# A graph network in three gather passes: blocks of many and of few columns set alternately

## Chip, cores and metric

The kernel runs on one core of a Trainium2 chip. The metric is the device time of one launch in microseconds (us); smaller is better. The core has five engines that run side by side: TensorE (PE in the profile, its weight loads PEld), VectorE (DVE), ScalarE (ACT), GpSimd (POOL) and SyncE (SP). GpSimd issues the gathers, SyncE most plain transfers.

## What is computed

A directed graph has 6250 nodes with 256 features each and 100000 edges sorted by target `dst`. Two GATv2 layers (4 heads of 64) with self loops, a residual and layer norm, then one GAT layer (8 heads of 32), again with residual and layer norm. Cut to what matters:

```python
def _gatv2_layer(x, src, dst, n, Wl, Wr, att, b):
    xl = (x @ Wl).reshape(n, H, C)
    xr = (x @ Wr).reshape(n, H, C)
    e = leaky_relu(xl[src] + xr[dst], 0.2)
    logits = einsum('ehc,hc->eh', e, att)
    alpha = softmax of logits over the edges of each dst
    return segment_sum(xl[src] * alpha[:, :, None], dst) + b
h = elu(gatv2(x, ...)); h = gatv2(h, ...); x = layernorm(x + h)
# GAT: Wh = x @ W, e = leaky_relu(s1[src] + s2[dst]), softmax over dst, weighted sum
x = layernorm(x + gat(x))
```

The costly part is `xl[src]` three times: a row of about 1 KB for each of 100000 edges in each layer.

## The kernel before

`make_plan` counts the edges of each node and sorts the nodes by falling degree. The place of a node in that order (`place`) is split into a partition (`place & 127`, `piece[:, 0]`) and a block (`place >> 7`, `piece[:, 1]`): 49 blocks of 128 nodes, one node to a partition. Since the nodes of a block have about the same degree, a block needs only as many *columns* (edges of a node, gathered side by side) as its largest node has. The function `columns` fixes these numbers from the expected distribution of degrees. They are, by block: 38, 25, 24, 23, 22, 21, 21, 20, 20, 20, 19 x4, 18 x4, 17 x4, 16 x5, 15 x5, 14 x5, 13 x4, 12 x3, 11, 11, 10, 10, 9. Block 0 is gathered with 27 columns, its few longer nodes in an extra gather (`few_row`). The sum over the blocks is 803 columns in each layer.

`tile_by_degree` then makes three passes over the 49 blocks. Passes 1 and 2 are `layer2(0, ...)` and `layer2(1, ...)`, pass 3 is the code behind them. For each block b a pass does, in the order of the program:

- `gather(b + 1)`: one indirect DMA on GpSimd for each column of the next block (line 1235). It fetches 128 rows of 1040 to 1056 bytes, one to a partition, from a table in HBM (`xl1_d`, `xl2_d` or `wh_d`; in the profile `xl_d` and `whs_d`). Their targets are tiles `g` of up to T = 9 rows, from a pool of nine buffers (`rowp`). A GATv2 block takes its columns and one own row, cut by `chunks` in equal parts of at most nine: 18 columns or more make three tiles (four for block 0), 17 or fewer make two. GpSimd works through this list in order. It stops where a tile's buffer is still in use by the block that held it nine tiles earlier. In pass 1 it also fetches node features for block b + 3 (line 1595).
- `ready(b + 1)`: the products of the block's own rows (pass 1) or a copy of rows loaded before (pass 2).
- `attend(b)`: VectorE makes the logits, three instructions for each tile (lines 1504 to 1506: max, product, sum), and the top (line 1374). ScalarE exponentiates (line 1381).
- `end(b - 1)`: VectorE takes the finished sum `acc` of the block before, from PSUM (line 1537), and normalizes it.
- reciprocal of the new denominators (line 1571; it comes once per block and is used below as the block's mark).
- `weighted_sum`: VectorE multiplies the tiles by the weights (line 1411). ScalarE does so for the last third of the columns, with one instruction for each column and head (line 1410). TensorE adds all columns up in PSUM by products with an identity (line 1418). Only then are the tiles free again.
- the rest of `finish` for block b - 1: transposes, products, and a write of the table rows for the next layer by SyncE.

In pass 3 the logits are short, and VectorE does the weighted sum too (lines 1433 and 1442); GpSimd writes the output rows with one indirect DMA for each block (line 1733).

At the end of a pass, `begin` gathers the first 14, 12 and 11 columns of blocks 0 to 2 of the next pass. It reads only rows of the first 45 blocks (`AHEAD`), so that it need not wait for the last four (`LATE = 4`). For this `sort_sources` sorts the sources of blocks 0 to 2 by place. Everything in `tile_by_degree` takes its number of columns from the list `cols` by block number and the nodes from the places.

Of the kernel before, what the change touches and what calls it, by code (L numbers as in the profile page):

```python
# [28 lines left out]
I32 = mybir.dt.int32  # L29
AF = mybir.ActivationFunctionType  # L30
OP = mybir.AluOpType
# [4 lines left out]
P = 128  # L36
# [4 lines left out]
RUNS = 64  # L41
EARLY = (14, 12, 11)
LATE = 4


def columns(E, N, NB):

    mean = E / N
    pmf = [math.exp(-mean)]
    for k in range(1, 200):
        pmf.append(pmf[-1] * mean / k)
    over, sd = [], []
    for c in range(199):
        p = sum(pmf[c + 1 :])
        g = sum((k - mean) * pmf[k] for k in range(c + 1, 200))
        over.append(N * p)  # L60
        sd.append(math.sqrt(max(N * (p * (1.0 - p) - g * g / mean), 0.0)))
    cols = []
    for b in range(NB):
        most = P * b
        cols.append(next(
            c for c in range(199) if (over[c] + 3.5 * sd[c] <= most if b else over[c] < 0.01)
        ))
    low = max((c for c in range(199) if N - over[c] <= P // 4), default=0)
    high = next(c for c in range(199) if over[c] <= P // 4)
    pmf += [0.0] * 200  # L70
    held = next(
        c for c in range(199)
        if N * sum((k - c) * pmf[k] for k in range(c, 200))
        + 3.5 * math.sqrt(N * sum((k - c) ** 2 * pmf[k] for k in range(c, 200))) <= P
    )
    assert cols[1] <= held < cols[0]
    return cols, low, high, held


@with_exitstack  # L80
# [566 lines left out]
def kernel(  # L647
# [20 lines left out]
    NB = -(-N // P)  # L668
    NP = NB * P
    cols, low, high, held = columns(E, N, NB)  # L670
    CM = max(cols)
    H2, D2 = att1.shape
# [18 lines left out]
    with tc.manual_schedule():  # L691
        make_plan(
            tc, x, src, dst, ((wl1, wr1, att1), (wl2, wr2, att2)), (b1, b2), w3, a3,
            cols, low, high, held, node_i, fits, ident, eps, nobody, att, wc, wh, fixed, xl1_d, near_d,
        )
        nc.vector.memset(done, 0)
# [18 lines left out]
def make_plan(  # L715
# [6 lines left out]
    nc = tc.nc  # L722
    N, F = x.shape
    E = src.shape[0]
    NB = node_i.shape[1]
# [12 lines left out]
    one = ctx.enter_context(tc.tile_pool(name="plan_one", bufs=1))  # L738
# [306 lines left out]
    place_f = one.tile([P, NB], F32, name="place_f")  # L1045
# [3 lines left out]
    piece = one.tile([P, 2, NB], I32, name="piece")  # L1049
    nc.vector.tensor_single_scalar(piece[:, 0, :], place, P - 1, op=OP.bitwise_and)  # L1050
    nc.vector.tensor_single_scalar(piece[:, 1, :], place, 7, op=OP.logical_shift_right)
    nc.vector.tensor_scalar(vals[:, 2, :], count, 255.0, None, op0=OP.min)
    to = one.tile([P, 2, NB], BF16, name="to")
    nc.vector.tensor_copy(to, piece)
# [88 lines left out]
def tile_by_degree(  # L1143
# [32 lines left out]

    AHEAD = (NB - LATE) * P
    KEY = max(cols).bit_length()
# [614 lines left out]
```

## Time and profile before

| what | value |
|---|---|
| time, median of 3 runs | 3889.89 us (3889.52 to 3891.73) |
| profiled execution | 3880.55 us |
| its span, first to last instruction | 3878.7 us |
| VectorE busy | 2836.2 us (73%) |
| GpSimd busy | 2530.5 us (65%) |
| TensorE busy, weight loads | 1481.8 us (38%), 1113.8 us (29%) |
| ScalarE busy | 1091.1 us (28%) |
| gathers of layers 1 and 2 | 1569 of 948 ns, 766 of 1036 ns in layer 3, and 2 x 37 early ones |
| data moved | 395.60 MB, 102 GB/s |
| mean granted TensorE clock | 0.665 |

The span has four parts. The plan and the first table last until 150 us. Pass 1 then runs until about 1500 us, pass 2 until about 2710 us, and pass 3 to the end. In lines of the profile, idle time of an engine stands behind the bar or in brackets, with what ended it. "issue" means that the profile shows nothing that it waited for; "remote" means that the releaser is not known. The times of TensorE's ends are modelled. The rows here come from one execution, whose own time is 3880.55 us.

### The profile page before, as it was taken

The page shows a single profiled execution, that of the slowest core. Times are in us where ns is not written, and L with a number is a line of the kernel's source. Part 1 is how long each engine was busy: PE and PEld are TensorE (multiplying, and loading weights), DVE is VectorE, ACT ScalarE, POOL GpSimd, SP SyncE. Part 2 cuts the span into 40 slices and gives each one's busy share as a digit, 9 for nine tenths or more (in the row PEclk, how much of TensorE's full clock was granted, in tenths as well). Part 3 has the DMA queues.
Part 4 walks back from the last instruction along what each step waited for, and adds up shares of the span by engine and source line. Part 5 has one row for each costly group of instructions (what it writes and reads, how often), then busy time and mean ns, then how long its engine had stood idle before and what let it go on. Part 6 is the DMA issues. An engine that isn't in the chain of part 4 may idle for free.

```text
span 3878.7 us, 23608 instructions
## 1 busy us (share of the span) xinstructions
PE 1481.8 (38%) x5130; PEld 1113.8 (29%) x5130; DVE 2836.2 (73%) x2648; ACT 1091.1 (28%) x4176; POOL 2530.5 (65%) x2613
## 2 busy tenths in 40 slices
PE   6324665556667763355544545554000000000000
PEld 5213444434555542343433433443000000000000
DVE  6228988668888876899876988896676565666665
ACT  3113444334445442243433434443000000000000
POOL 6464666666666645666666666664777777777774
PEclk8656877778788886676666677776555555555555
DMA  8532333333434334333433434442343333333332
GB/s 188 109 92 78 98 104 104 100 99 103 105 102 108 104 79 109 100 106 104 112 107 105 111 107 110 109 111 74 101 108 101 96 97 96 97 97 96 97 97 57
DMA packets 196123, 395.60 MB, mean 102 GB/s; under 512 B 63036, under 2 KB 115514, under 8 KB 195956
## 3 DMA queue, kind: packets, MB, share of 16 engines
q0 software_dynamic: 122048, 338.04, 33.2%
q1 hardware_dynamic: 66226, 54.22, 5.1%
q10 hardware_dynamic: 7698, 1.74, 0.4%
q8 instruction: 45, 0.74, 0.1%
q14 instruction: 106, 0.87, 0.1%
HBM read 353.82 MB, written 40.42 MB: 102 GB/s over the span
## 4 chain that ended last, share of the span: by engine, by line
issue 20%; POOL 20%; DVE 13%; PE 10%; another core or an unknown queue 6%; ACT 5%; DMA 1%; DVEq 0%; POOLq 0%; ACTq 0%
POOL g L1235 18%; PE acc L1418 6%; DVE z L1505 4%; DVE z L1504 4%; DVE lg L1506 3%; PE pm L1362 3%; ACT g L1410 2%; ACT wt L1381 2%; DVE g L1411 1%; POOL out L1733 1%; DMA g<-xl_d,near_r 1%; DVE weighted L1433 1%; ACT xT L1357 0%; PE pt L1355 0%
## 5 line engine op out<-in xcount | busy, mean ns | idle before, releaser
L1235 POOL DMA_INDIRECT g<-xl_d,near_r x1569 | 1487.4, 948 | 858.7 <-issue 454.3
L1418 PE MATMUL acc<-g,ident 128*128 128x256 f32 x3408 | 1015.9, 461 | 765.3 <-issue 282.7
L1418 PEld LDWEIGHTS acc<-g,ident 128*128 128x128 f32 x3408 | 774.4, 234 | 1004.2 <-issue 522.3
L1235 POOL DMA_INDIRECT g<-whs_d,near_r x766 | 793.2, 1036 | 284.2 <-issue 250.0
L1410 ACT ACTIVATE g<-g,by 128x64 f32<-128x64 f32 x2056 | 545.1, 337 | 316.1 <-issue 310.8
L1504 DVE TENSOR_TENSOR z<-g,pr 128x1820 f32<-128x1820 f32 (+4 forms) x234 | 497.1, 2125 | 19.1 <-DMA g<-xl_d,near_r 10.0
L1505 DVE TENSOR_TENSOR z<-z,at 128x1820 f32<-128x1820 f32 (+4 forms) x234 | 497.4, 2126 | 8.0
L1506 DVE TENSOR_REDUCE lg<-z 128x28 f32<-128x1820 f32 (+4 forms) x234 | 497.3, 2125 | 8.1
L1442 DVE TENSOR_REDUCE acc_v<-weighted 128x256 f32<-128x4096 f32 (+15 forms) x49 | 343.7, 7014 | 16.5 <-remote 8.3
L1411 DVE TENSOR_TENSOR g<-g,wt 128x1792 f32<-128x1792 f32 (+8 forms) x234 | 348.4, 1505 | 2.9
L1391 ACT ACTIVATE wt<-lg 128x128 f32<-128x128 f32 (+17 forms) x49 | 14.0, 285 | 851.0 <-DVE top L1374 391.5
L1703 DVE TENSOR_TENSOR lg<-g,s_r 128x56 f32<-128x56 f32 (+4 forms) x111 | 22.1, 213 | 315.1 <-DMA g<-whs_d,near_r 272.5
L1357 ACT COPY xT<-pt 128x256 f32<-128x256 f32 x147 | 54.9, 374 | 688.5 <-remote 342.2
L1433 DVE TENSOR_TENSOR weighted<-g,wt 128x1792 f32<-128x1792 f32 (+4 forms) x111 | 226.6, 2056 | 0.1
L1571 DVE RECIPROCAL den<-den 128x4 f32<-128x4 f32 x98 | 17.4, 177 | 212.9 <-ACT wt L1381 165.2
L1381 ACT ACTIVATE wt<-lg,top 128x19 f32<-128x19 f32 (+14 forms) x392 | 116.0, 296 | 190.8 <-DVE lg L1506 74.3
L1362 PE MATMUL pm<-wcat,xT 128*128 128x260 f32 x392 | 136.0, 505 | 56.3 <-ACT xT L1357 49.8
L1362 PE MATMUL pm<-wh_cat,xT 128*128 128x272 f32 x196 | 77.5, 531 | 183.8 <-ACT xT L1357 95.5
L1537 DVE TENSOR_TENSOR h<-acc,den 128x256 f32<-128x256 f32 x98 | 40.7, 416 | 126.2 <-remote 112.8
L1362 PEld LDWEIGHTS pm<-wcat,xT 128*128 128x128 f32 x392 | 94.8, 255 | 90.5 <-ACT xT L1357 64.6
L1362 PEld LDWEIGHTS pm<-wh_cat,xT 128*128 128x128 f32 x196 | 42.8, 242 | 203.0 <-ACT xT L1357 104.7
L1362 PE MATMUL pl<-wcat,xT 128*128 128x260 f32 x196 | 64.0, 455 | 55.5 <-issue 40.4
(232 smaller groups left out, 1548.4 us busy)
## 6 DMA issues: line engine op xcount, KB each, us to landing
g<-xl_d,near_r POOLq DMA_INDIRECT x1569
g<-whs_d,near_r POOLq DMA_INDIRECT x766
whs_d<-row SPq DMA_DIRECT2D x49, 132.0 KB
xl_d<-xl SPq DMA_DIRECT2D x49, 130.0 KB
xl_d<-row SPq DMA_DIRECT2D x49, 130.0 KB
xr_d<-row SPq DMA_DIRECT2D x49, 130.0 KB
two<-xl_d SPq DMA_DIRECT2D x49, 130.0 KB
two<-xr_d SPq DMA_DIRECT2D x49, 130.0 KB
```

What stands on the lines that cost most here:

```text
L1235: nc.gpsimd.indirect_dma_start(out=g[:, j + own - s0, :width], out_offset=None, in_=table, in_offset=source(of, b, j),)
L1357: nc.scalar.copy(xT, pt)
L1362: nc.tensor.matmul(pm, xT[:, c, :], w[:, c, :], start=c == 0, stop=c == 1)
L1381: nc.scalar.activation(wt[:, :, h], lg[:, :S, h], AF.Exp, bias=top[:, h : h + 1], accum_out=den[:, h : h + 1],)
L1410: nc.scalar.mul(g4[:, t, h, :], g4[:, t, h, :], by[:, t - m, h : h + 1])
L1411: nc.vector.tensor_mul(g4[:, :m], g4[:, :m], wt[:, s0 : s0 + m, :].unsqueeze(3).to_broadcast([P, m, H, F // H]),)
L1418: nc.tensor.matmul(acc, ident, g4[:, t], start=s0 + t == 0, stop=s0 + t == S - 1 and not more)
L1433: nc.vector.tensor_mul(prod[:, s0 - base : s1 - base, :].rearrange("p t (h d) -> p t h d", h=H), g[:, :n, :F].rearrange("p t (h d) -> p t ...
L1442: nc.vector.reduce_sum(part, prod[:, : s1 - base, :].rearrange("p s f -> p f s"), axis=AX.X)
L1504: nc.vector.tensor_max(z, g[:, :n, :W2], xr[:, None, :].to_broadcast([P, n, W2]))
L1505: nc.vector.tensor_mul(z, z, at[:, None, :].to_broadcast([P, n, W2]))
L1506: nc.vector.reduce_sum(lg[:, s0:s1, :], z.rearrange("p t (h d) -> p t h d", h=H2), axis=AX.X)
```

## The change

After the columns are worked out, the list is permuted: blocks 0 to 2 and the last four stay where they are. The 42 blocks between are laid out with a large and a small one by turns. By number of columns the order becomes 38, 25, 24, 23, 11, 22, 12, 21, 12, 21, 12, 20, 13, 20, 13, 20, 13, 19, 13, 19, 14, 19, 14, 19, 14, 18, 14, 18, 14, 18, 15, 18, 15, 17, 15, 17, 15, 17, 15, 17, 16, 16, 16, 16, 16, then 11, 10, 10, 9 as before. `make_plan` applies the same permutation to the block number of each node with ten small VectorE instructions, so that the places, and all tables written by place, follow. The blocks themselves (which nodes, how many columns, how many tiles) are the same, and nothing else is edited.

```diff
+FIRST = len(EARLY)
...
-    return cols, low, high, held
+    turns = cols[:]
+    for r in range(FIRST, NB - LATE):
+        turns[min(2 * r - FIRST, 2 * (NB - LATE) - 1 + FIRST - 2 * r)] = cols[r]
+    return turns, low, high, held
...
     nc.vector.tensor_single_scalar(piece[:, 1, :], place, 7, op=OP.logical_shift_right)
+    turn_a = one.tile([P, NB], I32, name="turn_a")
+    turn_b = one.tile([P, NB], I32, name="turn_b")
+    nc.vector.tensor_scalar(
+        turn_a, piece[:, 1, :], 2.0, float(-FIRST), op0=OP.mult, op1=OP.add
+    )
+    nc.vector.tensor_scalar(
+        turn_b, piece[:, 1, :], -2.0, float(2 * (NB - LATE) - 1 + FIRST), op0=OP.mult, op1=OP.add
+    )
+    nc.vector.tensor_tensor(turn_a, turn_a, turn_b, op=OP.min)
+    nc.vector.tensor_tensor(turn_a, turn_a, piece[:, 1, :], op=OP.subtract)
+    nc.vector.tensor_single_scalar(turn_b, piece[:, 1, :], float(FIRST), op=OP.is_ge)
+    nc.vector.tensor_tensor(turn_a, turn_a, turn_b, op=OP.mult)
+    nc.vector.tensor_single_scalar(turn_b, piece[:, 1, :], float(NB - LATE), op=OP.is_lt)
+    nc.vector.tensor_tensor(turn_a, turn_a, turn_b, op=OP.mult)
+    nc.vector.tensor_tensor(piece[:, 1, :], piece[:, 1, :], turn_a, op=OP.add)
+    nc.vector.scalar_tensor_tensor(
+        place_f, piece[:, 1, :], float(P), piece[:, 0, :], op0=OP.mult, op1=OP.add
+    )
```

## The prediction

> **What bounds the kernel now.** I read the page first, then the waits of GpSimd and VectorE pass by pass, then the timeline of a few blocks. The page:
>
> ```profile
> PE 1481.8 (38%) x5130; PEld 1113.8 (29%) x5130; DVE 2836.2 (73%) x2648; ACT 1091.1 (28%) x4176; POOL 2530.5 (65%) x2613
> L1235 POOL DMA_INDIRECT g<-xl_d,near_r x1569 | 1487.4, 948 | 858.7 <-issue 454.3
> L1235 POOL DMA_INDIRECT g<-whs_d,near_r x766 | 793.2, 1036 | 284.2 <-issue 250.0
> ```
>
> A gather costs GpSimd 0.95 us and 0.30 us until the next, so 1.25 us. VectorE is the busiest and GpSimd next; neither fills the span. The waits of GpSimd between 1567 and 2617 us (pass 2, the gathers of blocks 3 to 47) and of VectorE between 2773 and 3720 us (pass 3):
>
> ```profile
> POOL g L1235 <- issue: 200.0, 655, 0.6
> POOL g L1235 <- PE acc L1418: 96.2, 29, 6.0
> POOL g L1235 <- remote: 63.1, 18, 4.3
> ...
> DVE lg L1703 <- DMA g<-whs_d,near_r: 266.7, 34, 10.3
> ```
>
> In pass 2 GpSimd stands still for some 160 us, for tiles that TensorE still reads: about 3.5 us for each block. In pass 3 VectorE waits for rows: GpSimd is the bound, at 727 gathers and 46 outputs in 1060 us (2773 to 3833). The timeline of pass 2, from one block mark (L1571) to the next, block 9 of 20 columns:
>
> ```profile
> 1785.36 0.94 POOL L1235 DMA_INDIRECT g<-xl_d,near_r  x1 [3.69 <-remote]
> ...
> 1790.58 0.18 DVE L1571 RECIPROCAL den<-den 128x4 f32<-128x4 f32 x1 [1.67 <-ACT wt L1381]
> ...
> 1793.42 5.83 ACT L1410 ACTIVATE g<-g,by 128x64 f32<-128x64 f32 x24
> ...
> 1808.10 0.95 POOL L1235 DMA_INDIRECT g<-xl_d,near_r  x1 [0.30 <-issue]
> 1812.58 0.94 POOL L1235 DMA_INDIRECT g<-xl_d,near_r  x1 [3.54 <-remote]
> 1812.69 0.37 ACT L1357 COPY xT<-pt 128x256 f32<-128x256 f32 x1 [13.44 <-remote]
> ...
> 1814.02 0.41 DVE L1537 TENSOR_TENSOR h<-acc,den 128x256 f32<-128x256 f32 x1
> ...
> 1817.80 0.18 DVE L1571 RECIPROCAL den<-den 128x4 f32<-128x4 f32 x1 [2.23 <-ACT wt L1381]
> ```
>
> A block is a burst of 19 gathers (1785.4 to 1809.0) and a gap of 3.5 us. What ScalarE wanted from TensorE reaches it only in the gap, 13.4 us late, at the moment when GpSimd gets its tiles. So 27.2 us pass for 19 gathers, 1.43 us each, though VectorE is idle in only 2.2 us of them. After longer unbroken bursts, where two-tile blocks begin to follow three-tile ones, the delay is larger (block 17 of pass 2, 40.7 us between marks):
>
> ```profile
> 2032.29 0.95 POOL L1235 DMA_INDIRECT g<-xl_d,near_r  x1 [0.30 <-issue]
> 2037.06 0.94 POOL L1235 DMA_INDIRECT g<-xl_d,near_r  x1 [3.83 <-remote]
> ...
> 2040.42 0.42 DVE L1537 TENSOR_TENSOR h<-acc,den 128x256 f32<-128x256 f32 x1 [12.84 <-remote]
> ```
>
> In blocks of 12 columns the burst is 10 to 12 gathers, the gap 2.7 us and the distance of marks 16.5 us (2568.14 to 2584.67), 1.38 us for a column. So the price of a column is nearly the same in large and small blocks: gathers with their gaps set the pace, and VectorE (24.5 us busy in a block of 20 columns, 15.9 us in one of 12) fits beside them.
>
> **The change part by part.** The sums go against the execution's own 3880.55 us; the median of the runs is 9.3 us above it, so I add 9.3 at the end.
>
> *Ten instructions in the plan.* Their neighbours (L1048 to L1054, the same 128x49 shape) take 0.17 to 0.23 us, together 1.9 us ahead of the instruction at 52.43 us that builds the block's one-hots. GpSimd is gathering lists until 114 us and then idle for 35.7 us until the writes of `near_d` have landed; the fill that follows the lists is what VectorE waits for at 95 to 116 us. This cover hides them: 0, and 1.9 if it is gone.
>
> *VectorE against GpSimd.* Nothing is removed: the same 803 columns, 117 tiles and 49 blocks in a pass. A gain would need blocks where VectorE is late while GpSimd has nothing to do, and others the other way round. A pair of 20 and 12 columns costs 27.2 + 16.5 = 43.7 us before (1.37 a column); its VectorE time is 24.5 + 15.9 = 40.4. In turns the tile of a block is refilled by the one nine tiles later, so a large block frees three tiles for 20 or 21 gathers: 21 x 1.247 + 3.5 = 29.7 us. A small one frees two for 13: 13 x 1.247 + 2.0 = 18.2 us. That is 47.9 us for 34 gathers, 1.41 each: the rate of before, at most 1.5 us a pair above it. VectorE's order helps: when the sum of the large block is done, it is already at the logits of the next large one, so 24.5 us meet the 29.7 and 16 to 18 us the 18.2. I take 0 here and price that excess in the next part.
>
> *The chain under the short burst.* The 24 or 28 ScalarE instructions of a large block (L1410) now run in a burst of 13 gathers. In pass 1 they start 9.1 us after the burst does (553.24 against 544.1). The first twelve take 3.1 us, the others about 1.2 us each while the burst lasts (557.38 to 570.72), and 0.25 us where nothing disturbs them. The short burst of pass 1 has 14 requests, 17.5 us, so 16 or 17 of them are done in it. The rest takes 2 to 3 us, TensorE's tail 1.5: 3.5 to 4.4 us in place of a gap of 2.1 to 2.7. Excess 0.8 to 2.3, say 1.5 us for each of the 14 blocks with three tiles (22 to 18 columns): +21 in pass 1, from 0 to 32. In pass 2 the same instructions end in time where they run undisturbed (5.83 us above); they were slow in blocks 3 to 6 only, 4 of 14, so +6, from 0 to 32. The Trainium skill (SBUF — State Buffer, section Who interferes with whom) says that TensorE and ScalarE never wait for anyone at the SBUF ports; by that alone this part is 0 and the sum 10 us less. The row above, 18 us for 24 instructions beside gathers, speaks for another cause, and I go by it.
>
> *Pass 3.* In the middle GpSimd is the bound and stays so: a pair needs the same gathers, and VectorE needs 17.7 + 12.2 us of busy time for 20 and 12 columns against 26.4 + 16.8 us between marks. At the end it is different. From block 42 on all blocks are small, and VectorE falls behind: the mark of block 41 follows its last gather by 4.7 us, that of block 44 by 14.3, that of block 48 by 29.8 (3862.48 against 3832.7). With 16 columns before the last four the lag starts at 5 again and grows for four blocks only: by 15.5 at the pace of before (a gain of 9), by nothing if VectorE keeps up (25). I take -15.
>
> *Ends of the passes.* The first three and last four blocks, the early gathers and `AHEAD` are as before, so the 29 us for which VectorE waits at block 48 of pass 2, behind 37 early gathers without a break, stay: 0.
>
> Sum: 0 + 0 + 21 + 6 - 15 = +12. 3880.55 + 12 = 3892.6, and 9.3 more for the median: 3902 us.
>
> **The rivals.** *The long stalls go (faster).* The longest distances of marks in pass 1 (39.2 us at block 14, 45.3 at 18) and pass 2 (40.7 at 17, 43.6 at 19), three of the four at the border from three to two tiles, cost 9 + 20 + 11 + 21 = 61 us more than the blocks next to them. In turns, tile sizes mix from the start and there is no single border. If all of that goes, the chain costs nothing, and pass 3 gains 15: 3890 - 76 = 3814. Against it: the new order has many borders, one in each pair.
>
> *The bursts meet the wrong block (slower).* If TensorE's results pass only in the gaps, and VectorE begins the large block's logits only after the small block's mark, the burst of 29.7 us faces a small block (15.9 us) and that of 18.2 a large one (24.5): 29.7 + 24.5 = 54.2 us in place of 47.9, 6.3 for each of 14 pairs, 88 us in one pass and 176 in two: 3978 or 4066. It decides as soon as ScalarE's xT (L1357) waits for the gap in every small block. The 13.4 us above speak for it, the 0.3 us of idle VectorE in blocks of 12 columns against it.
>
> *It does nothing*: the gathers' rate rules in all passes and the last blocks of pass 3 lag as before: 3890. That the places do not follow the columns, so that the slow path runs, I see no reason for in the diff.
>
> **How the numbers follow.** My forecast (3902, own range 3880 to 3935) 0.46, the faster rival 0.30, the slower one 0.20, nothing 0.04. About 0.2% (8 us) is what this kernel's measurement can tell from no change. Faster: 0.30 and 0.04 of the forecast's lower end, 0.34. Same: 0.04 and 0.08 of the forecast, 0.12. Slower: the other 0.54. The range goes from the faster rival with pass 3 at its best (25 gained in place of 15: 3804) to one pass of the slower one with the chain at its dearest (3978 + 32: 4010), and leaves out some 0.10 on each side.
>
> **What would show it.** In the profile after: GpSimd's waits for TensorE in pass 2 near 160 us; marks of pass 1 and 2 some 28 to 32 us (small block, behind the long burst) and 18 to 23 us (large) apart; the last mark of pass 3 about 15 to 20 us behind the last gather. Wrong is the forecast if the middle of passes 1 and 2 (340 to 1415, 1621 to 2617 us) gets shorter or longer by over 40 us.

## The result, and the profile after

The changed kernel takes 3956.26 us (median of 6 runs, 3938.19 to 3964.93), the kernel before in the same session 3889.49 us: a ratio of 1.0169, 95% interval 1.0145 to 1.0193. It is slower by 66.8 us. The profiled execution took 3964.24 us with a span of 3962.4 us, so 83.7 us of span more than the profiled execution before (3878.7); it is one of the longest of its six.

From the marks of the two profiles (the reciprocal of each block, L1571 before and L1594 after) the 83.7 us divide like this:

| stretch | before | after | difference |
|---|---|---|---|
| start to mark of block 2, pass 1 | 339.6 | 343.6 | +4.0 |
| pass 1, mark of block 2 to mark of block 44 | 1075.0 | 1137.7 | +62.7 |
| to mark of block 2, pass 2 | 206.7 | 210.1 | +3.3 |
| pass 2, block 2 to block 44 | 995.6 | 1020.0 | +24.4 |
| to mark of block 2, pass 3 | 179.4 | 181.0 | +1.7 |
| pass 3, block 2 to block 48 | 1066.2 | 1050.2 | -16.0 |
| last mark to the end | 16.2 | 19.9 | +3.6 |

The page after, the lines that answer to those shown of before:

```profile
PE 1476.1 (37%) x5129; PEld 1114.5 (28%) x5130; DVE 2838.6 (72%) x2658; ACT 1087.4 (27%) x4176; POOL 2537.4 (64%) x2639
L1258 POOL DMA_INDIRECT g<-xl_d,near_r x1569 | 1489.3, 949 | 945.0 <-issue 460.1
L1258 POOL DMA_INDIRECT g<-whs_d,near_r x766 | 798.0, 1042 | 280.2 <-issue 245.3
```

No engine works longer. GpSimd has 86 us more idle time in front of its gathers of layers 1 and 2 (945.0 against 858.7): the time is lost in waits. The waits of GpSimd in pass 2 (1638 to 2711 us, the gathers of blocks 3 to 47) and of VectorE in pass 3 up to the mark of block 41:

```profile
POOL g L1258 <- issue: 203.7, 664, 1.1
POOL g L1258 <- PE acc L1441: 89.8, 21, 8.4
POOL g L1258 <- remote: 82.6, 23, 5.8
...
DVE lg L1726 <- DMA g<-whs_d,near_r: 180.2, 25, 12.8
```

GpSimd's waits in pass 2 are 172 us, near the 160 of before, as the prediction said. The new waits are VectorE's. Its waits in pass 1 between the marks of blocks 2 and 44, before (339.6 to 1414.6 us; us in total, times, longest) and after (343.6 to 1481.3 us):

```profile
DVE den L1571 <- ACT wt L1381: 103.0, 31, 12.1
...
DVE pr L1592 <- PE acc L1418: 3.2, 1, 3.2
```

```profile
DVE den L1594 <- ACT wt L1404: 55.8, 23, 5.7
DVE pr L1615 <- remote: 49.7, 7, 7.6
...
DVE h L1640 <- ACT neg L1632: 19.0, 4, 5.5
DVE pr L1615 <- DMA g<-xl_d,near_r: 14.7, 2, 7.6
DVE pr L1615 <- PE acc L1441: 13.1, 3, 6.8
DVE h L1640 <- ACT pos L1635: 13.1, 5, 5.3
```

The waits at `pr` (L1615) were one of 3.2 us before and are 79 us now. L1615 is the helper `none`: before VectorE begins the logits of the next block in pass 1, it pads the four heads of that block's right-hand rows `pr`, which TensorE makes (`own1`). Pass 2 has no such instruction: there ScalarE copies `pr` from rows that were padded when they were written. VectorE's waits make up the whole loss of both passes. All of them together, between the marks of pass 1, grow from 188.1 to 251.1 us, by 63.0, and pass 1 grows by 62.7; without them pass 1 lasts 886.9 us before and 886.6 after. The padding brings +75 and the wait for ScalarE at L1640 +31, while the wait at the mark (`den`) falls by 38. In pass 2 all waits grow from 118.6 to 143.8 us, by 25.2 where the pass grows by 24.4: +13.7 at the sum `acc` and +11.5 at the mark. One turn of the cycle, from the timeline of pass 1 (blocks 14 and 15, of 13 and 20 columns):

```profile
689.84 0.82 PE L1385 MATMUL pr<-wcat,xT 128*128 128x260 f32 x3
...
690.25 0.18 DVE L1594 RECIPROCAL den<-den 128x4 f32<-128x4 f32 x1 [1.86 <-issue]
...
702.02 0.95 POOL L1258 DMA_INDIRECT g<-xl_d,near_r  x1 [0.30 <-issue]
...
705.89 0.06 DVE L1615 MEMSET pr<- 128x4 f32 x1 [6.80 <-remote]
...
707.55 0.94 POOL L1258 DMA_INDIRECT g<-xl_d,near_r  x1 [4.58 <-remote]
...
727.05 0.18 DVE L1594 RECIPROCAL den<-den 128x4 f32<-128x4 f32 x1 [0.73 <-ACT wt L1404]
...
728.96 5.82 ACT L1433 ACTIVATE g<-g,by 128x64 f32<-128x64 f32 x24
...
735.91 0.95 POOL L1258 DMA_INDIRECT g<-xl_d,near_r  x1 [11.14 <-PE acc L1441]
```

TensorE has made `pr` of the large block by 690.7 us. GpSimd is in a burst of 20 gathers until 703.0. VectorE has nothing else to do from 699.1 us on, but the padding starts only at 705.9, in the pause behind that burst, and the 18.8 us of the large block's logits follow it. So the large block's mark comes 36.8 us behind the small one's. Meanwhile GpSimd has done its burst of 14 and stands still for 11.1 us, because tiles come free only when the large block's sum is made. Then the next long burst begins, and the padding of the next large block waits in it. Twelve paddings of pass 1 wait for more than 1 us. They start 7 to 17 us after TensorE has made `pr`, seven of them 1 to 4 us behind a long burst, the other five 1 to 7 us before its end. So the result is seen late in or behind a long burst, not in the pause alone.

### The profile page after: what moved, and what is told of

It reads as the page before. It is cut to its first block, busy times and chain, and to the rows that moved or that the text cites. A ratio compares the mean times of both kernels' runs of the same rounds, so it can differ in the third digit from the quotient of the medians.

```text
span 3962.4 us, 23662 instructions
## 1 busy us (share of the span) xinstructions
PE 1476.1 (37%) x5129; PEld 1114.5 (28%) x5130; DVE 2838.6 (72%) x2658; ACT 1087.4 (27%) x4176; POOL 2537.4 (64%) x2639
## 4 chain that ended last, share of the span: by engine, by line
issue 23%; POOL 19%; DVE 18%; PE 10%; another core or an unknown queue 9%; ACT 7%; DMA 2%; DVEq 0%; POOLq 0%; ACTq 0%
POOL g L1258 18%; PE acc L1441 7%; DVE z L1527 5%; DVE z L1528 5%; DVE lg L1529 4%; ACT g L1433 3%; ACT wt L1404 2%; PE pm L1385 2%; DVE g L1434 1%; DMA g<-xl_d,near_r 1%; POOL out L1756 1%; DVE weighted L1456 1%; ACT xT L1380 0%; DVE top L1397 0%
## 5 line engine op out<-in xcount | busy, mean ns | idle before, releaser
L1258 POOL DMA_INDIRECT g<-xl_d,near_r x1569 | 1489.3, 949 | 945.0 <-issue 460.1
L1434 DVE TENSOR_TENSOR g<-g,wt 128x1792 f32<-128x1792 f32 (+6 forms) x234 | 348.3, 1505 | 2.9
L1414 ACT ACTIVATE wt<-lg 128x112 f32<-128x112 f32 (+17 forms) x49 | 14.0, 285 | 779.3 <-DVE lg L1413 274.6
L1404 ACT ACTIVATE wt<-lg,top 128x15 f32<-128x15 f32 (+15 forms) x392 | 115.8, 295 | 271.3 <-DVE lg L1529 95.8
L1594 DVE RECIPROCAL den<-den 128x4 f32<-128x4 f32 x98 | 17.4, 178 | 198.7 <-ACT wt L1404 139.8
L1385 PE MATMUL pm<-wcat,xT 128*128 128x260 f32 x392 | 125.6, 474 | 57.9 <-ACT xT L1380 39.9
```

The lines of the kernel that those rows point to most:

```text
L1258: nc.gpsimd.indirect_dma_start(out=g[:, j + own - s0, :width], out_offset=None, in_=table, in_offset=source(of, b, j),)
L1385: nc.tensor.matmul(pm, xT[:, c, :], w[:, c, :], start=c == 0, stop=c == 1)
L1404: nc.scalar.activation(wt[:, :, h], lg[:, :S, h], AF.Exp, bias=top[:, h : h + 1], accum_out=den[:, h : h + 1],)
L1434: nc.vector.tensor_mul(g4[:, :m], g4[:, :m], wt[:, s0 : s0 + m, :].unsqueeze(3).to_broadcast([P, m, H, F // H]),)
```

## The experiments

*The parts of the change, each by itself.* In the kernel before, a pass can take its blocks in any order, whatever their places are; only the first three and the last four matter to the early gathers.

```diff
 # turns_pass1: pass 1; turns_pass2: i == 1; turns_pass3: the loop of pass 3
+        order = (by_turns(NB)) if i == 0 else (list(range(NB)))
...
-            for b in range(NB):
+            for k, b in enumerate(order):
...
-                if b + 1 < NB:
-                    gather(b + 1)
+                if k + 1 < NB:
+                    gather(order[k + 1])
 # plan_only, against the changed kernel
-        turns[min(2 * r - FIRST, 2 * (NB - LATE) - 1 + FIRST - 2 * r)] = cols[r]
+        turns[r] = cols[r]
-    nc.vector.tensor_single_scalar(turn_b, piece[:, 1, :], float(NB - LATE), op=OP.is_lt)
+    nc.vector.tensor_single_scalar(turn_b, piece[:, 1, :], 0.0, op=OP.is_lt)
```

plan_only:

> The ten added VectorE instructions alone, with a condition that is never met, so that every block keeps its place. The marks of the first block show 4.0 us more in the profile after than in the profile before (205.8 against 201.8). If the instructions cause that: 3893 us and the first mark near 206. If it is the new order of the nodes in the tables (or chance): 3890 and the first mark near 202.

turns_pass1:

> Places, tables and lists as before; only pass 1 takes its blocks in the order by turns (block 4's successor by rank and so on, the same order of columns as in the change). If the loss comes from the order in which a pass works and pass 1 bears +63 of it as the marks say: 3953 us, marks from block 2 to the 45th 1138 us apart (1075 before), passes 2 and 3 as before. If the loss comes from the places (which rows of the tables are read, and in which pattern): 3890.

turns_pass2:

> As turns_pass1, with the order by turns in pass 2 alone. By the marks of the two profiles: +24, 3914 us. If TensorE's part in the next block's right-hand rows (pass 1 only) is what a long burst holds up, pass 2 has no such wait and stays within 0 to 30. If it is something that all GATv2 blocks share: +60.

turns_pass3:

> As turns_pass1, with the order by turns in pass 3 alone. By the marks and by the prediction's step on the end of pass 3: -16, 3874 us, the last mark 14 us behind the last gather. If pass 3 gains only because something earlier was shifted: 3890.

Measured together on one chip, on which the kernel before takes 3867.96 us:

| kernel | median us | ratio | 95% interval | the stretch, from its profile |
|---|---|---|---|---|
| plan_only | 3874.53 | 1.0009 | 0.999 to 1.0028 | first mark 203.5 |
| turns_pass1 | 3898.21 | 1.0074 | 1.005 to 1.0098 | pass 1: 1093.2 |
| turns_pass2 | 3897.67 | 1.0077 | 1.0051 to 1.0103 | pass 2: 1023.0 |
| turns_pass3 | 3858.11 | 0.9967 | 0.9944 to 0.999 | pass 3: 1050.7 |

The stretches that these four leave in the order of degrees last 1061.2 to 1084.0 us in pass 1, 980.8 to 986.5 in pass 2 and 1064.8 to 1066.2 in pass 3. So the order in which passes 1 and 2 work costs about 30 us in each, the order of pass 3 gains 10 by the medians and 13 by the ratio (16 between the marks), and the ten instructions cost nothing that can be measured. That the loss lies in the order and not in the places is shown for most of it: the four add up to 1.27%, of the 1.69% measured. The missing 0.42% is no more than these five ratios leave uncertain together, but the profiles point to a real part in it. In the profile after, pass 1 is 44 us longer than in turns_pass1, with the same order of columns, and after_pause, a kernel further below with the changed places, shows a pass 1 as long as that again. In the profile after the cycle described above goes on to block 26, in turns_pass1 it ends at block 14, and from there a pair takes 50 us. Why is open. The order of degrees in the changed tables, which would tell whether the places have a part in it, was not run.

VectorE's waits in turns_pass1 between the same marks of pass 1, and in turns_pass2 of pass 2:

```profile
DVE pr L1600 <- remote: 20.6, 3, 7.1
DVE pr L1600 <- issue: 13.0, 2, 6.8
```

```profile
DVE h L1545 <- remote: 61.2, 10, 12.1
DVE h L1545 <- PE acc L1425: 15.1, 3, 7.3
```

In pass 1 the wait at the padding is back (34 us). In pass 2 the wait that grows is the one for the sum `acc` (L1545): 76 us in 13 waits, 70 us in 11 in the profile after, and 36 to 56 us in 4 to 7 in the profiles of these chips where pass 2 keeps the order of degrees. Both are waits of VectorE for something that TensorE makes. The sums of pass 2 are not all late in the same way. In the profiles before (1621.3 to 2616.9 us) and after (1691.3 to 2711.3):

```profile
DVE h L1537 <- remote: 53.7, 6, 18.8
DVE h L1537 <- PE acc L1418: 2.5, 1, 2.5
```

```profile
DVE h L1560 <- remote: 40.5, 6, 10.9
DVE h L1560 <- PE acc L1441: 18.9, 3, 7.0
```

In the three waits of the last line TensorE itself ends just before VectorE reads: the 24 ScalarE instructions of blocks 21, 25 and 29 took 14.8 to 16.9 us beside a burst, so the sum was made late, and not only seen late.

The expectations that follow speak of three theories. Theory 1: beside a long burst TensorE's results reach VectorE late. Theory 2: ScalarE's scaling is slow beside gathers, so tiles come free late. Theory 3: nine buffers are too few for the mixed sizes.

*The wait at the padding taken away.* VectorE reads a fixed tile, so it need not wait for TensorE, and pass 1 leaves the right-hand rows out of its logits.

```diff
                 rows, cut, xr = state.pop(b)
+                if i == 0 and b:
+                    xr = at
...
-                if i == 0 and b + 1 < NB:
-                    none(state[b + 1][2])
```

turns1_fixed:

> Order by turns in pass 1 alone, and in pass 1 the logits of blocks 1 to 48 read a fixed tile in PSUM in place of the block's own right-hand rows; TensorE still makes these rows, but VectorE neither pads nor reads them (so pass 1 leaves the right-hand rows out of its logits). To be read against before_fixed. Theory 1: with that wait gone (34 to 79 us) pass 1 by turns is at most 15 us longer than pass 1 of before_fixed, unless the wait moves to the sum acc (then 15 to 40). Theories 2 and 3: pass 1 stays 20 to 60 us longer.

before_fixed:

> The order of before with the same fixed tile in pass 1: there the padding waited for 0 to 3 us only, so all theories expect 3860 to 3895 us, pass 1 1060 to 1085 between the marks.

Measured on a second chip (kernel before 3869.33 us): turns1_fixed 3883.16 us, ratio 1.0034 (1.0015 to 1.0053); before_fixed 3869.84 us, 0.9996 (0.9972 to 1.002). Pass 1 lasts 1087.0 and 1081.2 us. With that wait gone, the order by turns in pass 1 costs 13 us in the medians and 6 between the marks, where it had cost 30 in the medians and 9 to 32 between the marks. That is what theory 1 expects (at most 15 us), not theories 2 and 3 (20 to 60). Blocks 5 to 14, five pairs, take 256 us in place of 276 in turns_pass1 and 283 in the profile after. VectorE's waits in pass 1 of turns1_fixed:

```profile
DVE den L1581 <- ACT wt L1388: 110.2, 25, 14.2
DVE den L1581 <- issue: 49.1, 16, 5.7
DVE h L1547 <- remote: 29.4, 5, 9.7
```

By the medians the padding accounts for about half of the loss in pass 1. This share is not clear of noise: the loss of the one pair of kernels is 0.74% (0.50 to 0.98), that of the other 0.38%, uncertain by 0.3. Part of the time came back as waits at the mark (159 us against 126 in turns_pass1). The fixed tile in the changed kernel was not run on these two chips.

*A pause behind each gather.* If results pile up because gathers come too closely, a slower pace should free them.

```diff
                     in_offset=source(of, b, j),
                 )
+                for _ in range(pause):
+                    nc.gpsimd.memset(gap_t, 0.0)
```

There is one memset behind each gather. The tile is 128x1 here, and 128x416 in the long form further below.

after_pause:

> The changed kernel with a GpSimd memset of 128x1 (0.13 us in pass 3 of the profile) behind each gather of passes 1 and 2, so that a gather takes about 1.4 us in place of 1.25 and a burst never runs unbroken. Theory 1 (in a long unbroken burst TensorE's results reach VectorE only in the next pause; the waits at the padding of the next block's right-hand rows, 79 us in pass 1, and at the sum acc, 70 us in pass 2, are of that kind): these waits fall under 20 us each, passes 1 and 2 get shorter by 30 to 90 us together, 3870 to 3925 us. Theory 2 (ScalarE's scaling is slow beside gathers, the tiles come free late) and theory 3 (nine buffers are too few for the mixed sizes): nothing is taken away and some 1400 gathers cost 0.13 to 0.2 us more, of which a part hides in the gaps: 4000 to 4150 us.

before_pause:

> The same pause in the kernel before. Theory 1: VectorE's waits for the sum acc (34 to 47 us in pass 1, 40 to 56 in pass 2) fall under 15 each; the rest of the order had little to lose: 3800 to 3860 us. Theories 2 and 3: 3930 to 4050 us.

Measured beside the two above: after_pause 3956.0 us, 1.022 (1.017 to 1.0269); before_pause 3876.61 us, 1.0026 (1.0 to 1.0052). These two tell nothing on the theories, because the memset takes 0.12 us and fits into the 0.30 us between two gathers: their distance stayed 1.25 us. What they show is that the loss repeats: pass 1 of after_pause lasts 1139.4 us, with 95 us of waits at the padding, and pass 2 1017.0.

*The last four.* The long pause, the changed kernel without the padding's wait, and a freer order of pass 3 were run on a third chip, on which the kernel before takes 3370.96 us (3367.49 to 3374.9), 13% less than on the others.

```diff
 # apart_pass3, pass 3 alone
+        order = list(range(3)) + ends_apart(NB)   # 3, 47, 4, 46, 5, 45, ... 24, 25, 26, 48
```

after_fixed:

> The changed kernel with the fixed tile in pass 1, as in turns1_fixed (pass 1 leaves the right-hand rows out of its logits). In the profile after, pass 1 runs from block 5 to 26 in a cycle of 55 to 60 us for two blocks: a burst of 21 gathers, a wait at the padding until it ends, the logits of the large block, and GpSimd idle for 10 to 12 us meanwhile. Theory 1 (the wait at the padding starts this cycle): pass 1 between the marks falls from 1138 to 1075 to 1100 us, GpSimd has no gaps of 10 us behind bursts of 14, 3900 to 3930 us in all. Theory 2 (ScalarE's scaling): pass 1 stays over 1120.

after_pause_long:

> As after_pause, with a memset of 128x416 (by 0.52 us for 128x512 in the profile, 0.43) in place of 128x1, which went into the 0.30 us between two gathers and left their distance at 1.25 us. Expected distance 1.38 to 1.5 us. Theory 1 in its form that results pile up because gathers come at 1.25 us and are worked off at 1.40 (the distance in pass 3): waits at the padding under 20 us, at the sum under 25, passes 1 and 2 at 1060 to 1100 and 980 to 1010 us, 3880 to 3930 in all. In its form that any unbroken row of gathers holds results up whatever its pace: the waits stay at 70 to 100 and passes 1 and 2 get longer by 20 to 100 each, 4000 to 4150.

apart_pass3:

> Pass 3 alone in another order: nothing gathers behind it, so the last four need not be last. Blocks 3 to 47 by turns (23, 10, 22, 10, 21, 11, ... 16, 16), the block of 9 columns last. In the change the lag of the mark behind the last gather grew from 5 us to 14 over the last three small blocks. If the prediction's step on pass 3 is right (VectorE falls behind only where small blocks follow each other): lag at the last mark 5 to 8 us, pass 3 another 6 to 10 us shorter than by turns, 20 to 26 in all: 0.993 to 0.995 of the kernel before. If the lag at the end is set by the last blocks whatever precedes them: as turns_pass3, 0.997.

apart3_pause:

> apart_pass3 with the pause of after_pause_long in passes 1 and 2, blocks there in the order of before. If results pile up at 1.25 us and not at 1.4: VectorE's waits for the sum (34 to 54 us in pass 1, 40 to 56 in pass 2) fall under 20, and it is 20 to 50 us faster than apart_pass3. If any row of gathers holds them up: 20 to 150 us slower than it.

Measured: after_fixed 3371.71 us, 1.0004 (0.9995 to 1.0013); apart_pass3 3372.07 us, 1.0002 (0.9993 to 1.0011); after_pause_long 3812.5 us, 1.1307 (1.129 to 1.1324); apart3_pause 3810.65 us, 1.1302 (1.1286 to 1.1317). None of the four expectations fits as a whole, since the delays that they are about were not seen on this chip. VectorE's waits in pass 1 of apart_pass3 (order of degrees, 260 to 1176 us) and in pass 2 of after_fixed (order by turns, 1353 to 2247 us), whole answers:

```profile
DVE den L1582 <- ACT wt L1392: 28.6, 41, 0.7
DVE bad L1360 <- PE pb L1358: 0.7, 1, 0.7
```

```profile
DVE den L1596 <- ACT wt L1404: 18.4, 43, 1.4
```

No wait for the sum and none at the padding, though GpSimd never pauses in pass 1 of apart_pass3: 730 requests in a row at 1.25 us. A mark and a padding in the midst of them (timeline of apart_pass3):

```profile
575.05 0.95 POOL L1246 DMA_INDIRECT g<-xl_d,near_r  x1 [0.30 <-issue]
575.54 0.18 DVE L1582 RECIPROCAL den<-den 128x4 f32<-128x4 f32 x1 [0.72 <-ACT wt L1392]
...
577.38 5.82 ACT L1421 ACTIVATE g<-g,by 128x64 f32<-128x64 f32 x24
...
579.93 0.06 DVE L1603 MEMSET pr<- 128x4 f32 x1
...
580.29 0.95 POOL L1246 DMA_INDIRECT g<-xl_d,near_r  x1 [0.30 <-issue]
```

So a long burst does not hold up results by itself; on the chips of the other sessions results came late beside one. There the order by turns costs 30 us in pass 2; here pass 2 lasts 893.1 us by turns (after_fixed) and 891.4 by degrees (apart_pass3). VectorE's waits in it are 18 and 15 us here, 119 in the profile before and 144 in the profile after, and without them the pass lasts 875 to 877 us in all four. This is the clearest evidence that the loss of pass 2 is made of late results. It speaks against theory 3 as well: the same nine buffers with the same mix of sizes lose nothing here. That the changed kernel as it stands would lose nothing on this chip is likely but wasn't run: in after_fixed pass 1 has no padding. Pass 3 needs 953.8 us by turns and 955.4 in the freer order, with the last mark 5.7 and 7.3 us behind the last gather; the whole kernel is level with the one before, so there seems to be no lag to take away on this chip (the kernel before was not profiled on it), and what the freer order would bring on the others stays open.

The long pause can't tell the theories apart where nothing is late. It shows its own price: the memset takes 0.46 us, the distance of two gathers becomes 1.57 us, and VectorE, which is the bound of pass 2 here and level with GpSimd in pass 1, waits for rows instead (221 us in pass 1 and 157 in pass 2 of after_pause_long); passes 1 and 2 last 1135.2 and 1051.5 us.

A version that beats both kernels is turns_pass3, the order by turns in pass 3 alone: 0.9967 (0.9944 to 0.999) of the kernel before.

## Why the prediction was right or wrong

The range of 3804 to 4010 us holds the measured 3956, and the direction is right, but the forecast of 3902 us, with its own 3880 to 3935, is not the case that came true. It summed +12; the medians differ by +66.8 and the profiled spans by +83.7. Its own sign of being wrong, the middle of passes 1 and 2 longer by over 40 us, appeared (+62.7 and +24.4).

- *What sets the pace:* the prediction read the pace of passes 1 and 2 as that of the gathers with their gaps, into which VectorE fits. But VectorE has the same work in every profile that keeps the padding, some 887 us in pass 1 and 877 in pass 2, and in pass 2 that is more than its 680 gathers need at 1.25 us (850 us). Only VectorE's waits differ: on the third chip they are 15 us, and pass 2 takes 891 us with the same gathers. The row of 13.44 us is also not a delay of 13.4 us: that is ScalarE's idle time, and TensorE had made the transposes 8.4 us before ScalarE read them (by the modelled ends).
- *The plan's ten instructions, 0:* right within what can be measured (1.0009, 0.999 to 1.0028). The first mark varies by 9 us between profiles of any order (197.6 in before_fixed, 206.9 in turns1_fixed), so the 4.0 us of the table say nothing.
- *VectorE against GpSimd, 0:* this is the step that failed. It took it that VectorE is already at the next large block's logits when a sum is done, so that 24.5 us meet the long burst. In pass 1 these logits begin with the padding, which waits for TensorE, and TensorE's result was seen only near the end of the long burst or behind it. Large blocks came out at 24 to 48 us between marks and small ones at 20 to 23, where 18 to 23 and 28 to 32 were predicted. Fourteen pairs (blocks 5 to 32) took 777.2 us, 55.5 us a pair. That is near the 54.2 us of the slower rival and not the 47.9 of the forecast. In pass 2, which has no padding, they took 684.6 us, 48.9 a pair, near the forecast's 47.9, though not in its pattern (large 22 to 36 us, small 18 to 32). The loss is there all the same, +24 in the profile and some 30 in the runs, because the pair of before was taken too low: 43.7 us is a pair of blocks without stalls, while the 42 blocks between the marks averaged 51.2 us a pair in pass 1 and 47.4 in pass 2 (1075.0 and 995.6 us), against 54.2 and 48.6 after.
- *The chain under the short burst, +21 and +6:* the size of this part was nearer to the truth than its reason. In pass 1 after, ScalarE's 24 or 28 instructions took 5.8 to 9.3 us in the large blocks 5 to 25, not the 18 us of before, since most of them ran while GpSimd stood still. From block 27 on they took 13 to 15 us in all large blocks but one. In pass 2 the chain was there, in the three waits of 18.9 us shown above. The rule of the Trainium skill that I set aside (SBUF — State Buffer, Who interferes with whom: TensorE and ScalarE wait for no one) agrees with the third chip: the same 24 instructions took 5.8 us in every such block there, beside gathers without a break. So gathers alone don't make the 18 us of before; that late signals do is likely, and not shown. By the rule alone this part is 0 and the sum 27 us less (21 + 6), not the 10 that the prediction states.
- *Pass 3, -15:* right: -16.0 between the marks, the last mark 14.2 us behind the last gather (15 to 20 predicted, 29.8 before), and 0.9967 when done alone. 3.6 us of it were given back behind the last mark.
- *The slower rival* is nearest in mechanism, in one pass of two, and names the wrong place: not xT (L1357) in the small block, but the padding in front of the large one. Its 3978 us left out the gain of pass 3; with the 15 us it would be 3963, beside the measured median of 3956. That is close in part by luck: it charged 88 us to one pass, and the profile shows 62.7 in pass 1 and 24.4 in pass 2.
- *The faster rival:* the long stalls did not go. Pass 1 after still has one of 48.0 us, pass 2 waits of up to 10.9 us for the sum.

## What to carry to other kernels

Before blocks are reordered so that loads even out, list for each engine the first instruction of a block that needs another engine's result, in each pass by itself: in pass 1 here it was the padding of four columns. In these runs the time at which results were seen mattered more than how evenly the loads were spread, and the mean rate per column (1.37 to 1.41 us) says nothing about it. An order can be given to each pass alone, and the pass that is bound by transfers can gain from one that costs the others.

## What was not expected of the hardware

- One chip ran the same kernel in 3371 us and two others in 3868 and 3869 us. The packets of the gather queue took as long on both kinds: 33.2% of 3878.7 us is 1288 us in the profile before, 38.4% of 3371.3 us is 1295 us in apart_pass3, by the line of the profile `q0 software_dynamic`. GpSimd issued at the same 1.25 us. What differs is how soon results are seen: VectorE's waits for the sums and at the padding were 0 on the one, between the marks of blocks 2 and 44, and up to 107 us (79 + 28, pass 1 after) on the others. TensorE's products of the sums (L1418) took a median of 379 ns on both, so slower products are not the reason. Why is open.
- On the slower kind the distance of gathers in pass 3 grows to a median of 1.28 us, on the other it stays 1.25; pass 3 takes 1066 against about 955 us.
- A GpSimd memset of 0.12 us behind each gather is free (distance 1.25 us); one of 0.46 us makes it 1.57 us.
